# Two cross-attention layers: sharing one value product between two entries by turning every other entry's key order round

## The chip, the cores and the metric

The kernel runs on one core of a Trainium2 chip. The metric is the device time in microseconds of one execution; the time before is the median of three runs. A core has five engines that run their own instruction streams in order and wait for each other by semaphores: TensorE (PE, matrix products; its weight loads are shown as PEld), VectorE (DVE), ScalarE (ACT), GpSimd (POOL) and SyncE (SP), which here only issues DMAs.

## The reference

Sixteen batch entries go through two cross-attention layers. In the first one, which the change is about (the code counts it as layer 0), each entry has 256 queries of 320 channels (20 heads of 16) and 256 context rows of 512. The first 77 rows are text, the other 179 are image tokens.

```
q = hidden_states @ Wq
k_text, v_text = text @ Wk, text @ Wv;  ip_k, ip_v = ip @ Wk_ip, ip @ Wv_ip
probs = softmax(q_h @ k_h^T * scale)                      # per head, over the 77 text rows
text_out = probs @ v_h
text_probs = softmax(q @ k_text^T * scale)                # over all channels at once
sem = (text_probs @ text) @ ip^T * scale
ip_probs = softmax(q_h @ ip_k_h^T * scale + 0.5 * sem) * spatial_mask   # over the 179 image rows
out = (text_out + ip_probs @ ip_v_h) @ Wout + bout + residual
```

The second layer is of the same kind, with 252 text rows and 4 image rows and a normalised semantic term.

## The kernel before

Products are made in three terms: each fp32 operand is split into a rounded half ("high") and the rest ("low"), and high x high, high x low and low x high are added. `prod` (L240) issues these as 12 matmuls when 512 rows of contraction are four tiles of 128. ACT makes the high half with a copy, DVE or POOL the low half with a subtraction (`halves`, `split`, `evacuate`, `in_turn`).

Context is loaded for two entries at once (a pair, number c), four tiles (`cta`, `cta`, `ctb`, `ctb`) of 128 x 512, each for 128 of the 512 context channels, columns in the order text, image of the first entry, then of the second. From it come per pair the keys (`keys0`, `keys_first` for pair 0: text keys with weights `wk0` in `wA`, image keys with `wki0` in `wB`), and per entry:

- the values (`values0_`): three groups of `prod` with 128 context rows on the output's rows and 320 value columns. Group 0 is the text (weights `wC`, rows 0 to 127), group 1 is the image weights (`wD`) on the same rows 0 to 127, group 2 is the image weights on rows 128 to 255. Group 0 and 1 are masked by `tmask` (row below 77, or from 77 on) as ACT copies them into `vr`; so text and image share the first tile of 128 keys, the mixed tile;
- the text x image product `M` (`tokens0`, 77 x 179, made 192 wide) for the semantic term, and from it with the text probabilities `tph` a second use in `semantic0`.

The heads are worked on in groups of four, NG = 5 groups an entry, one group a slot, 80 slots k = 0 to 79 in the first layer. In slot k PE makes scores for the maxima (`score0`, L745, two slots ahead; DVE reduces them, L746 and L747), turns the maxima round (`maxima0`, L753), makes transposed scores (`turned0`, L769, keys on the rows, two tiles t = 0 and 1) which ACT exponentiates (L772) and POOL multiplies by the semantic factor `rs` (L775), and for slot k-1 sums the values (`attend0`, L804). `settle0` normalises on DVE and adds text and image parts on POOL into `hsn` (L822); after the fifth group POOL also copies the last half column block beside itself (L824), since the last 64 channels stand twice for the three-term product of the output. `gather` then transposes and `close0` projects (`ho`, L610).

The stacked operands `ks` and `qs` hold the keys and queries of four heads with 80 more rows (M and indicators for the semantic term, or maxima). They come by DMA from DRAM copies `kd` and `qd`, written from `kst` and `q`. There are four of each in turn, so a slot's stack is loaded four slots ahead. The queries of an entry (`queries0`) begin with a split of x into `hq` (L283 to L285), whose third low half DVE makes with a multiply-add.

The order on PE is written by hand: slots call their parts in turn, and `task` gives each step of the other work a due time in slots, which `fill` obeys. The start (`begin`) is written by hand for every engine; after it the compiler's scheduler orders ACT, DVE, POOL and SP.

Of the kernel before, what the change touches and what calls it, by code (L numbers as in the profile page):

```python
# [17 lines left out]
S = 256  # L18
H = 20
# [16 lines left out]
CH = H * D  # L36

# [14 lines left out]
def xattn2(  # L52
# [60 lines left out]
    words, slots = {"ctb": 1024, "cta": 1024, "raw": 512, "rawc": 512, "both": 2 * (S - T0), "kb": 936, "si": 256, "sp": 128, "wC": 2 * 4 * (H * D + NIP), "mt": S, "mx": 2, "tmp": (NG + 1) * 48, "kst": 4 * S, "rs": 2 * S, "P": 4 * S}, {}  # L113
# [47 lines left out]
    def halves(hi, lo, src, eng=nc.vector, loaded=False):  # L161
        order = queued if loaded else lambda inst: inst
        if len(hi.shape) != len(src.shape):
            src = src.rearrange("p (d h) -> p d h", d=D)[:, :, :H]
# [26 lines left out]
    def in_turn(parts, wait, tag="raw", eng=nc.vector, later=False):  # L191

        ahead, parts, tags = [], list(parts), tag.split()
        for i in range(len(parts) + 1):
# [4 lines left out]
            if i:  # L199
                halves(*ahead.pop(0), eng, wait)  # L200
# [52 lines left out]
    def evacuate(hi, lo, out, m):  # L253

        if m < 2:
            return halves(hi, lo, out)
        hi, lo = hi[:64], lo[:64]
        both = buf("both", list(hi.shape), bufs=2)
        nc.scalar.copy(hi, out[:64])
        nc.scalar.copy(both, out[64:])  # L260
        nc.vector.tensor_sub(out[:64], out[:64], f(hi))
        nc.vector.tensor_add(lo, out[:64], both)

    def context(b, n, wait=0):

        tiles, parts = [], []
        for k in range(0, 4, 3 - n):
            src = cT_d[:, b * S : (b + n) * S].rearrange("(k p) t -> p k t", p=128)[:, k : k + 3 - n]
            ct = buf("cta" if n == 1 or k < 2 else "ctb", [128, 2, 512], FR, bufs=SIZES["CTA" if n == 1 or k < 2 else "CTB"], name="ct")
            split = lambda t: t.rearrange("p (k t) -> p k t", t=n * S)  # L270
            parts.append((src, split(ct[:, 0]), split(ct[:, 1])))
            tiles.append(ct)
        yield from in_turn(parts, wait, "rawc raw" if b == 2 and n == 2 else "rawc", nc.gpsimd if wait and b != 2 else nc.vector, n == 2 and b > 2)
        if n == 2:
            return lambda s, k: tiles[k][:, s].rearrange("p (b t) -> p b t", b=2)
# [3 lines left out]
    def split(src, neg, eng, tag):  # L279
# [5 lines left out]
        order(nc.vector.scalar_tensor_tensor(hl[:, 2], f(hl[:, 2]), neg, src[:, 2], op0=ALU.mult, op1=ALU.add))  # L285
        return hl

    ct = [buf(t, [128, 2, 512], FR, bufs=2, name="ct") for t in ("cta", "cta", "ctb", "ctb")]
    ct0 = {0: lambda s, k, tiles=ct: tiles[k][:, s].rearrange("p (b t) -> p b t", b=2)}
# [10 lines left out]
    for k in range(4):  # L300
        first["c", k] = cT_d[k * 128 : (k + 1) * 128, : 2 * S], ct[k][:, 0], ct[k][:, 1], ("rawc", "raw")[k // 2]
# [8 lines left out]
    ks = [const_tile([128, 4, S], f"ks{i}", FR) for i in range(SIZES["NR"])]  # L310
# [8 lines left out]
    def constants():  # L319
# [3 lines left out]
        for i in range(SIZES["NR"]):  # L323
            nc.gpsimd.memset(f(ks[i]), 0.0)
# [1139 lines left out]
```

## Time and profile before

| | |
|---|---|
| median of 3 runs (range) | 1501.86 us (1500.63 to 1506.5) |
| profiled execution, its span | 1499.52 us, 1497.7 us |
| busy PE, DVE, ACT, POOL | 95%, 78%, 59%, 81% of the span |
| granted PE clock, mean | 0.984 |
| first layer's attention begins, at about | 56 us |
| PE busy from 300 to 400 us, and from 600 to 700 | 98.14 and 85.17 us of 100 |

The rows of the profile name the line of the kernel, the engine, the operation, output and input tiles and their shapes. "Idle before" is the time the engine stood still ahead of the instruction, with what released it. Matmuls overlap, so what one costs is read from the distance of two starts, not from its own duration.

### The profile page before, as it was taken

Reading aid. Unit: us, or ns where it says so; the run is one execution under the profiler, and the core shown is the slowest. Engines: PE = TensorE matmul, PEld = TensorE weight load, DVE = VectorE, ACT = ScalarE, POOL = GpSimd, SP = SyncE. Lnnn points to the kernel's source line nnn. Section 1 sums busy time; section 2 is a strip of 40 time slices with the busy share of each in tenths; the row PEclk is TensorE's granted clock in tenths of the full one; section 3 lists DMA queues with packets and bytes.
Section 4 is the critical chain, followed back from the end, with each engine's and each line's share of the span. In section 5 each row is a group of like instructions: output and inputs, shape, how many; then the busy total and the mean of one; then the engine's idle time right before and its main releaser. Section 6 shows DMA issues by size and latency. Waiting matters only on the chain.

```text
span 1497.7 us, 36123 instructions
## 1 busy us (share of the span) xinstructions
PE 1427.8 (95%) x12740; PEld 1155.6 (77%) x12740; DVE 1170.2 (78%) x2593; ACT 884.8 (59%) x1975; POOL 1215.2 (81%) x1304
## 2 busy tenths in 40 slices
PE   8789999999999899789999999999999999999997
PEld 8678888888888778577777777777777777777765
DVE  5467777777777787878887788778877887788785
ACT  5346565656565555556666666666666666666562
POOL 4259797979797977887698879887988798879786
PEclk9799999999999999999999999999999999999999
DMA  7767787778787776775434434443444344433411
GB/s 237 201 185 217 201 228 200 217 206 224 199 231 193 219 200 173 186 216 150 145 102 132 127 108 128 127 127 108 127 128 127 109 126 129 127 108 103 122 26 39
DMA packets 230986, 234.32 MB, mean 156 GB/s; under 512 B 39127, under 2 KB 200678, under 8 KB 230790
## 3 DMA queue, kind: packets, MB, share of 16 engines
q1 hardware_dynamic: 228598, 230.71, 55.4%
q8 instruction: 102, 1.67, 0.5%
q10 hardware_dynamic: 2208, 1.30, 0.4%
q14 instruction: 78, 0.64, 0.1%
HBM read 118.04 MB, written 77.04 MB: 130 GB/s over the span
## 4 chain that ended last, share of the span: by engine, by line
PE 73%; DVE 8%; DMA 6%; POOL 6%; issue 3%; ACT 3%; SPq 1%; ACTq 0%; DVEq 0%; POOLq 0%
PE X L942 15%; PE X L240 14%; PE P L804 6%; PE X L610 5%; PE P L954 5%; PE S L745 5%; PE P L964 4%; PE T L769 4%; PE T L894 3%; PE S L900 3%; PE X L613 2%; PE X L250 2%; PE X L579 2%; POOL P L775 2%; DVE mn L747 1%
## 5 line engine op out<-in xcount | busy, mean ns | idle before, releaser
L775 POOL TENSOR_TENSOR P<-P,rs 128x512 f32<-128x512 f32 x320 | 414.4, 1318 | 90.2 <-ACT P L772 89.3
L933 POOL TENSOR_TENSOR wt<-P,ctb 128x512 f32<-128x512 f32 x320 | 410.6, 1308 | 72.8 <-ACT ctb L932 72.8
L942 PE MATMUL X<-ctb,gm 128*128 128x512 f32 x1120 | 305.4, 402 | 5.8 <-DVE wt L943 5.7
L772 ACT ACTIVATE P<-T 128x512 f32<-128x512 f32 x320 | 175.4, 594 | 159.5 <-PE T L769 101.9
L943 DVE TENSOR_TENSOR wt<-X,wt 128x512 f32<-128x512 f32 x320 | 216.1, 680 | 42.7 <-PE X L942 36.4
L942 PEld LDWEIGHTS X<-ctb,gm 128*128 128x128 f32 x1120 | 195.3, 188 | 39.0 <-DVE wt L943 8.7
L914 ACT ACTIVATE P<-T 128x512 f32<-128x512 f32 x320 | 173.0, 593 | 76.2 <-PE T L894 73.3
L932 ACT ACTIVATE ctb<-P 128x512 fp32r<-128x512 f32 x320 | 186.7, 627 | 36.8 <-PE X L942 33.1
L902 DVE TENSOR_REDUCE mn<-S 128x4 fp32r<-128x1008 f32 x160 | 191.3, 1196 | 0.0
L747 DVE TENSOR_REDUCE mn<-S 128x4 fp32r<-128x716 f32 x160 | 142.2, 889 | 0.0
L804 PE MATMUL P<-P,vr 128*32 128x256 f32 x1920 | 127.4, 396 | 5.3 <-DVE tmp L821 2.0
L745 PE MATMUL S<-ks,qs 125*128 125x256 f32 x640 | 117.7, 307 | 4.9 <-DMA ks<-M 2.8
L745 PEld LDWEIGHTS S<-ks,qs 125*128 125x128 f32 x640 | 89.0, 195 | 40.1 <-issue 20.9
L1031 POOL TENSOR_TENSOR r<-u,rs 128x40 f32<-128x40 f32 (+2 forms) x17 | 108.7, 6394 | 3.9 <-DVE u L1028 3.9
L769 PE MATMUL T<-qs,ks 127*128 127x256 f32 x640 | 108.2, 292 | 0.4 <-DMA qs<-mt 0.4
L746 DVE TENSOR_REDUCE mn<-S 128x4 fp32r<-128x308 f32 x160 | 74.4, 465 | 31.2 <-PE S L745 30.8
L815 DVE STREAM_TRANSPOSE nt<-P 128x512 f32<-128x512 f32 x80 | 56.9, 711 | 51.8 <-PE P L804 51.3
L769 PEld LDWEIGHTS T<-qs,ks 127*128 127x128 f32 x640 | 92.1, 198 | 2.0 <-DMA qs<-mt 1.0
L804 PEld LDWEIGHTS P<-P,vr 128*32 128x32 f32 x1920 | 57.2, 112 | 47.0 <-issue 8.1
L954 PE MATMUL P<-P,v1t 128*32 128x256 f32 x1280 | 85.7, 385 | 0.0
L964 PE MATMUL P<-wt,zone 128*32 128x256 f32 x1280 | 85.1, 381 | 0.3 <-DVE wt L943 0.3
L610 PE MATMUL X<-ho,wF 128*128 128x256 f32 x512 | 74.3, 287 | 6.5 <-ACT mt L755 4.0
(297 smaller groups left out, 2974.5 us busy)
## 6 DMA issues: line engine op xcount, KB each, us to landing
qd<-q SPq DMA_DIRECT2D x96, 256.0 KB
qs<-tph SPq DMA_DIRECT2D x64, 320.0 KB
rawc<-in_cT_dram SPq DMA_DIRECT2D x60, 256.0 KB
qs<-qd SPq DMA_DIRECT2D x80, 192.0 KB
ks<-kd SPq DMA_DIRECT2D x80, 192.0 KB
ks<-kd SPq DMA_DIRECT2D x160, 96.0 KB
qs<-qd SPq DMA_DIRECT2D x160, 96.0 KB
kd<-kst SPq DMA_DIRECT2D x57, 256.0 KB
```

The costliest lines, as they stand in the source:

```text
L240: last = mm(out, lhs(a, k), rhs(b, k), start=i == 0, stop=i == len(terms) - 1)
L745: mm(sp[:, h], Q[: XROW + T0, h, t * 128 : (t + 1) * 128], K[: XROW + T0, h], start=True, stop=True)
L769: mm(st[p][:, j], K[:KS0, 2 * p + j, t * 128 : (t + 1) * 128], Q[:KS0, 2 * p + j], start=True, stop=True)
L772: exp = anchor(nc.scalar.activation(pt, st[p], AF.Exp, scale=SCALE))
L775: anchor(nc.gpsimd.tensor_mul(pt, pt, rs[:, t : t + 1].to_broadcast([128, 2, S])))
L804: mm(pv[32 * s : 32 * s + 32, o : o + S], v[:, vt, h : h + 32], P[k, s // 2][:, t, s % 2], start=vt < 2, stop=vt != 1,)
L902: anchor(nc.vector.tensor_reduce(maxes[k + 2][:, t], sp[:, :, :T1], axis=AX.X, op=ALU.max))
L914: anchor(nc.scalar.activation(P[k, u][:, t], st[u], AF.Exp, scale=SCALE))
L932: nc.scalar.activation(R[k, u][:, t], P[k, u][:, t], AF.Copy, scale=0.5)
L933: anchor(nc.gpsimd.tensor_sub(W[k, u][:, t], P[k, u][:, t], f(R[k, u][:, t])))
L942: mm(yp, gm[:, gb], R[k, u][:, kt], start=i == 0, stop=i == len(blocks[n]) - 1)
L943: nc.vector.tensor_mul(W[k, u][:, n], yp, W[k, u][:, n])
```

## The change

Nothing that is computed changes. Entries of even number get their keys, values and scores in the order image, text; odd ones keep text, image. A context tile is laid out as 51 zero columns, then for the high and then the low half: text of both entries (154), image of the even entry (179), a gap of 26 zeros, image of the odd entry (179), one zero. Rows 128 to 178 of the even entry's image, the gap, and rows 0 to 50 of the odd entry's image now lie 128 in a row, so one group of `prod` (`values_mixed`, task `vm`) makes the image values of both mixed tiles; ACT copies its result twice, with the mask of each entry. The even entry's mask is a new tile `emask`; the mask column of `vr` is written for each entry (`mark`) and no longer once at the start (`marks`). The keys' stack serves both orders from the same bytes, as one text block more stands behind the four heads (`turned_ks`), whose indicator rows need one more DMA for each of the four stacks at the start. `M` is laid out so that its zero columns are written once, and it is made 180 wide.

Since a layout has gaps, some operations come in two pieces: the halves of a context tile (text, image), the image part of a key's evacuation (each entry), the copy of the text keys to `kt`. Apart from that, `settle0` makes the last group's sum twice wide on DVE (in the second layer `settle1` its product), so POOL's copy (and in the first layer its add) goes, and for x the third low half of 64 rows moves from DVE to POOL.

```diff
+MIX = S - T0 - 128
+CI = 2 * T0
+CG = 128 + T0
+CW = CI + CG + S - T0 + 1
...
-    def evacuate(hi, lo, out, m):
+    def evacuate(hi, lo, out, m, pieces=None):
+        cut = [lambda t, b=b: t[:, b] for b in pieces] if pieces else [lambda t: t]
...
+        for of in cut:
+            nc.scalar.copy(of(hi), of(out[:64] if m == 2 else out))
...
+    def side(t, s, at, n):
+        at += MIX + s * CW
+        return t[:, at : at + n]
+    def texts_of(t, s):
+        return side(t, s, 0, CI).rearrange("p (b t) -> p b t", b=2)
+    def images_of(t, s, more=0):
+        return side(t, s, CW - 2 * CG, 2 * CG).rearrange("p (b t) -> p b t", b=2)[:, :, CG - S + T0 - 1 : CG - 1 + more]
...
+        if neg is None:
+            order(eng.tensor_sub(hl[64:, 2], src[64:, 2], f(hl[64:, 2])))
+        else:
+            order(nc.vector.scalar_tensor_tensor(hl[:, 2], f(hl[:, 2]), neg, src[:, 2], op0=ALU.mult, op1=ALU.add))
...
-    ks = [const_tile([128, 4, S], f"ks{i}", FR) for i in range(SIZES["NR"])]
+    ksw = [const_tile([128, 4 * S + T0], f"ks{i}", FR) for i in range(SIZES["NR"])]
+    ks = [by_head(t[:, : 4 * S]) for t in ksw]
+    turned_ks = [by_head(t[:, T0:]) for t in ksw]
...
+        for t in ct:
+            nc.gpsimd.memset(f(t[:, :MIX]), 0.0)
+            for s in range(2):
+                nc.gpsimd.memset(f(side(t, s, CI + S - T0, CG - S + T0)), 0.0)
+                nc.gpsimd.memset(f(side(t, s, CW - 1, 1)), 0.0)
...
+    def mark(b):
+        V = vr[(b + 2) % 3]
+        for t, m in enumerate(masks(b)):
+            nc.gpsimd.tensor_copy(vcols(V, V0W)[:, t, :, 16], m.to_broadcast([128, H]))
+        return V
...
             dma(ks[i][XROW + T0 : KS0, :, :T0], ind0r[:2, :T0].unsqueeze(1).to_broadcast([2, 4, T0]))
+            dma(ksw[i][XROW + T0 : KS0, 4 * S :], ind0r[:2, :T0])
...
-            for w, lo, hi, a, z in ((wk0, 0, T0 + 1, 0, T0), (wki0, T0 - 1, S, T0, S)):
+            for w, of, t in ((wk0, texts_of, T0), (wki0, lambda t, s: images_of(t, s, 1), S - T0 + 1)):
...
-        for t, (w,), lo, sc in ((0, wv0, 0, tmask[:, 0:1]), (1, wvi0, 0, tmask[:, 1:2]), (2, wvi0, 128, 1.0)):
+        value_rows(ct, T0 if i else -MIX, wv0[0], (V, 0, masks(b)[0]))
+        yield
+        value_rows(ct, CI + (CG + MIX if i else 0), wvi0[0], (V, 2, 1.0))
...
+    def values_mixed(c):
+        to = [(vr[(b + 2) % 3], 1, masks(b)[1]) for b in (2 * c, 2 * c + 1)]
+        value_rows(ct0[c], CI + 128, wvi0[0], *to)
+        yield
...
-        nc.gpsimd.memset(f(M[:, :, :T0]), 0.0)
-        prod(gp[:T0, : S - lo], lambda s, k: ct(s, k)[:, i, :T0], lambda s, k: ct(s, k)[:, i, lo:S], 4)
+        prod(gp[:T0, : S - T0 + 1], lambda s, k: texts_of(ct[k], s)[:, i], lambda s, k: images_of(ct[k], s, 1)[:, i], 4)
...
-        xs = split(x, tmask[:, 5:6], nc.gpsimd, "hq") if b else xs0.pop()
+        xs = split(x, None, nc.gpsimd, "hq") if b else xs0.pop()
...
-        Q, K = QK[k] = qs[k % SIZES["NR"]], ks[k % SIZES["NR"]]
+        Q, K = QK[k] = qs[k % SIZES["NR"]], (ks if b % 2 else turned_ks)[k % SIZES["NR"]]
...
-        for vt in range(3):
-            values0(k, pv, v, vt)
+        get("vm", b // 2)
+        for step in ((0, 0, 0, 1, 1), (1, 0, S, 1, 0), (2, 1, S, 0, 1)) if b % 2 else ((2, 0, S, 1, 0), (1, 1, S, 0, 1), (0, 1, 0, 1, 1)):
+            values0(k, pv, v, *step)
...
-        nc.gpsimd.tensor_add(hn[:, g // 2, :, g % 2], tmp[:, 0], tmp[:, 1])
         if g == NG - 1:
-            nc.gpsimd.tensor_copy(hn[:, 2, :, 1], hn[:, 2, :, 0])
+            nc.vector.tensor_add(hn[:, 2], *[tmp[:, i].unsqueeze(2).to_broadcast([128, 8, 2, 16]) for i in range(2)])
             later(0.45, lambda: gather(0, b))
+        else:
+            nc.gpsimd.tensor_add(hn[:, g // 2, :, g % 2], tmp[:, 0], tmp[:, 1])
...
-        task(("v0", 2 * c), shifted(n, -7, -5.4, -5), lambda b=2 * c: values0_(b), *k)
-        task(("v0", 2 * c + 1), shifted(n, -4, -3.8, -3.4), lambda b=2 * c + 1: values0_(b), *k)
+        task(("v0", 2 * c), shifted(n, -7, -5.4), lambda b=2 * c: values0_(b), *k)
+        task(("vm", c), shifted(n, -4.2), lambda c=c: values_mixed(c), *k)
+        task(("v0", 2 * c + 1), shifted(n, -3.8, -3.4), lambda b=2 * c + 1: values0_(b), ("vm", c))
```

How it moves instructions, at three places. On PE, in pair 4, between a slot's second `turned0` (output T) and the next slot's maxima (`ident_r`); wD is the image value weights, cta and ctb the context tiles. Before:

```order
737 L769 MATMUL T<-qs_97,ks_101 128x256 x4
738 L240 MATMUL X<-wD,cta_81 128x320 x3
739 L240 MATMUL X<-wD,cta_82 128x320 x3
740 L240 MATMUL X<-wD,ctb_83 128x320 x3
741 L240 MATMUL X<-wD,ctb_84 128x320 x3
742 L240 MATMUL X<-wD,cta_81 128x320 x3
743 L240 MATMUL X<-wD,cta_82 128x320 x3
744 L240 MATMUL X<-wD,ctb_83 128x320 x3
745 L240 MATMUL X<-wD,ctb_84 128x320 x3
746 L753 MATMUL X<-ident_r,mn_566 8x128 x2
```

And now (line numbers are those of the changed kernel):

```order
721 L864 MATMUL T<-qs_97,ks_101 128x256 x4
722 L251 MATMUL X<-wD,cta_81 128x320 x3
723 L251 MATMUL X<-wD,cta_82 128x320 x3
724 L251 MATMUL X<-wD,ctb_83 128x320 x3
725 L251 MATMUL X<-wD,ctb_84 128x320 x3
726 L848 MATMUL X<-ident_r,mn_614 8x128 x2
```

One of two groups is gone; the rest of PE's order around it stays, but that the odd entry's text group and the shared group change places a slot later.

On POOL, at the end of an entry (hq is the split of the next queries, P the probabilities, hsn the output being gathered). Before:

```order
260 L775 TENSOR_TENSOR P_122<-P_122,rs_115 128x512
261 L775 TENSOR_TENSOR P_123<-P_123,rs_115 128x512
262 L284 TENSOR_TENSOR hq_230<-xq_91,hq_230 128x512
263 L822 TENSOR_TENSOR hsn<-tmp_807 128x8x16
264 L775 TENSOR_TENSOR P_120<-P_120,rs_115 128x512
265 L775 TENSOR_TENSOR P_121<-P_121,rs_115 128x512
266 L824 COPY hsn<-hsn 128x8x16
267 L435 MEMSET M_260 77x2x77
268 L775 TENSOR_TENSOR P_120<-P_120,rs_115 128x512
```

And now:

```order
299 L397 COPY vr<-tmask 128x20 x2
300 L870 TENSOR_TENSOR P_123<-P_123,rs_116 128x512
301 L870 TENSOR_TENSOR P_124<-P_124,rs_116 128x512
302 L326 TENSOR_TENSOR hq_270<-xq_91,hq_270 128x512
303 L328 TENSOR_TENSOR hq_270<-xq_91,hq_270 64x256
304 L870 TENSOR_TENSOR P_121<-P_121,rs_116 128x512
305 L870 TENSOR_TENSOR P_122<-P_122,rs_116 128x512
306 L870 TENSOR_TENSOR P_121<-P_121,rs_116 128x512
```

The add, the copy and the memset are gone; two mark copies and the third low half stand there.

On ACT, its first copies in `begin`, with what they wait for (DMAHW: a load; Pool: GpSimd). Before:

```order
2 L1260 CAST cta_81<-rawc_117 128x512 [waits DMAHW0_49]
3 L1260 CAST wA_85<-P_120 128x320 [waits DMAHW1_49]
4 L1260 CAST cta_82<-rawc_118 128x512 [waits DMAHW2_49]
5 L1260 CAST wA_85<-P_121 128x320 [waits DMAHW3_49]
6 L1260 CAST ctb_83<-raw 128x512 [waits DMAHW4_49]
```

And now:

```order
2 L1359 CAST cta_81<-rawc_118 128x154 [waits DMAHW0_49]
3 L1359 CAST cta_81<-rawc_118 128x2x179 [waits Pool_49]
4 L1359 CAST wA_85<-P_121 128x320 [waits DMAHW1_49]
5 L1359 CAST cta_82<-rawc_119 128x154 [waits DMAHW2_49]
6 L1359 CAST cta_82<-rawc_119 128x2x179 [waits Pool_49]
```

Each context tile's copy is two, and the image one waits for POOL, which clears the gaps of that tile.

179 lines of the change are left out of this document (112 added, 67 removed).

## Prediction

> **What bounds the kernel now.** I read the page first (busy time), then the busy time by stretches, then what TensorE (PE) waited for, then the order of time on PE and GpSimd (POOL) in one period of the first layer, at last the first 60 us.
>
> ```profile
> span 1497.7 us, 36123 instructions
> PE 1427.8 (95%) x12740; PEld 1155.6 (77%) x12740; DVE 1170.2 (78%) x2593; ACT 884.8 (59%) x1975; POOL 1215.2 (81%) x1304
> ```
> ```profile
> 300.00:400.00 100.00, 98.14 (x933) 85.36 (x933) 78.11 (x182) 57.74 (x135) 85.61 (x84) 1.00 0.75 208
> ...
> 500.00:600.00 100.00, 91.32 (x842) 76.78 (x841) 81.77 (x183) 52.90 (x128) 80.71 (x89) 0.98 0.72 198
> 600.00:700.00 100.00, 85.17 (x785) 66.32 (x785) 77.20 (x173) 56.90 (x129) 86.58 (x100) 0.93 0.69 188
> ...
> 48.00:52.00 4.00, 2.33 (x17) 1.87 (x16) 1.29 (x2) 0.50 (x2) 0.23 (x1) 1.00 1.08 322
> 52.00:56.00 4.00, 0.47 (x3) 0.47 (x4) 3.10 (x6) 2.59 (x5) 0.00 (x0) 0.79 0.71 244
> ...
> 64.00:68.00 4.00, 4.00 (x27) 3.38 (x30) 1.32 (x3) 1.37 (x3) 2.01 (x2) 0.50 0.97 240
> ```
> The columns are the stretch, its length, busy us of PE, weight loads, VectorE (DVE), ScalarE (ACT) and POOL, the granted clock, DMA share and GB/s. From about 105 to 500 us, for which the first row stands, PE is busy all but 2%; from 500 to 700 it idles a tenth to a sixth; before 60 us it starves, and after the hole at 52 the clock is halved. What PE waits for in the dense part and in the hole-ridden one:
>
> ```profile
> PE X L610 <- ACT mt L755: 0.8, 1, 0.8
> PE X L240 <- DVE sp L670: 0.6, 1, 0.6
> PE X L667 <- DVE q L262: 0.3, 1, 0.3
> ```
> ```profile
> PE X L753 <- DVE mn L747: 4.2, 6, 1.7
> ```
> The first three rows are all of 200 to 300 us (1.7 us in 100), the last leads 500 to 600. So in the dense part each us taken off PE is a us of the kernel, if the engines that feed PE can follow; elsewhere it need not be.
>
> **The change, part by part.** One period of the dense part (a pair of entries), on PE:
>
> ```profile
> 262.54 1.13 PE L240 MATMUL X<-wC,cta 128*128 128x320 f32 x6
> ...
> 329.50 1.05 PE L240 MATMUL X<-wD,cta 128*128 128x320 f32 x6
> ...
> 332.15 1.04 PE L240 MATMUL X<-wD,ctb 128*128 128x320 f32 x6
> 333.03 0.28 PE L753 MATMUL X<-ident_r,mn 128*8 128x128 f32 x2
> ...
> 334.15 0.70 PE L240 MATMUL X<-cta 128*77 128x192 f32 x6
> 334.69 0.69 PE L240 MATMUL X<-ctb 128*77 128x192 f32 x6
> ...
> 337.94 1.13 PE L240 MATMUL X<-wC,cta 128*128 128x320 f32 x6
> ```
> A period is 337.94 - 262.54 = 75.4 us. 1) One value group of 12 matmuls goes per pair. From 329.50 to 333.03 stand two groups, so one is 3.53 / 2 = 1.765 us (not 12 times a matmul's own duration, since they overlap). Pairs 1 to 6 have it in the dense part: 6 x 1.765 = 10.6 us. Pair 7's lies at about 555 us, among PE's waits: between 0 and 1.8, taken as 0.9. Pair 0's lies at 46 us, ahead of the hole: nothing, that hole grows by it.
> 2) The token products go from 192 to 180 columns. Six take 334.69 - 334.15 = 0.54 us, 0.090 each; between no gain and full proportion (0.0056), taken at 0.005 x 12 x 14 entries = 0.8 us. Text keys from 156 to 154 columns: nothing.
> 3) POOL. Its rows, with those of DVE for the parts that change engines:
>
> ```profile
> L284 POOL TENSOR_TENSOR hq<-xq,hq 128x512 fp32r<-128x512 f32 x31 | 42.6, 1376 | 5.7 <-ACT hq L283 5.7
> L822 POOL TENSOR_TENSOR hsn<-tmp 128x128 f32<-128x128 f32 x80 | 41.0, 513 | 5.6 <-DVE tmp L821 5.1 <-DVE mx L674 0.5
> L824 POOL COPY hsn<-hsn 128x128 f32<-128x128 f32 x16 | 4.8, 300 | 0.1
> L435 POOL MEMSET M<- 77x154 f32 x16 | 3.6, 226 | 21.2 <-PE X L697 21.0
> L334 POOL COPY vr<-tmask 128x20 f32<-128x20 f32 x6 | 1.4, 302 | 3.9 <-DMA tmask<-in_tmask_dram 3.9
> ```
> ```profile
> L285 DVE SCALAR_TENSOR_TENSOR ho<-ho,tmask,hT 128x256 fp32r<-128x256 f32 x32 | 39.0, 1220 | 0.0
> L285 DVE SCALAR_TENSOR_TENSOR hq<-hq,tmask,xq 128x256 fp32r<-128x256 f32 x32 | 19.8, 618 | 2.3 <-ACT hq L283 1.9
> L168 DVE TENSOR_TENSOR q<-X,q 128x256 fp32r<-128x256 f32 x62 | 25.2, 415 | 12.1 <-ACT q L165 11.7
> ```
> Per pair POOL gains: two third low halves (256 columns; between 513 and 1376, by their middle width 0.8) = 1.6; four mark copies at 1.4 / 6 = 0.24: 1.0; each of four context tiles in two pieces (a line through 513 at 128 and 1376 at 512 has a foot of 0.23, so +0.2 each): 0.9; three key copies more: +0.2 each, 0.6. It loses two adds, two copies, two memsets: 2 x (0.51 + 0.30 + 0.23) = 2.1. Net +2.0 us on the 85.61 x 0.754 = 64.5 us of a period: 66.5 of 73.6, or 90%. POOL stays below PE on average, and its own waits are the cover. I look at where the cover is thinnest:
>
> ```profile
> 292.74 5.03 POOL L775 TENSOR_TENSOR P<-P,rs 128x512 f32<-128x512 f32 x4
> ```
> ```profile
> 298.17 1.50 PE L804 MATMUL P<-P,vr 128*32 128x256 f32 x24
> ```
> These four end at 297.77, and PE's attention starts 0.40 later; but its last 8 of 24 matmuls alone read the last two tiles, so the real slack is 0.40 + 1.50 x 16 / 24 = 1.4 us. In the run-up POOL now has one third low half and two half key copies more (0.8 + 0.3 or so). It fits, so I take 0; the bound is all of the 10.6. Even entries now read the late tiles after 8 matmuls instead of 16, which costs them 0.5 us of slack; in their slots POOL has idle time.
> 4) DVE loses 15 third halves (0.62 each) and gains 16 adds of 256 columns and three image pieces per pair (about 0.15 each), and in the second layer a doubled multiply. The add reads two SBUF tiles: between 0.42 (the q row, one input from PSUM) and 1.2 (the ho row, same size, both from SBUF); I take 0.8, so +7 us of DVE (16 x 0.8 + 24 x 0.15 - 15 x 0.62) where it is 78% busy. PE waits for DVE only from 500 to 700, with some 5 adds there: -1 to +3 us, taken as +0.5. The Trainium skill (SBUF — State Buffer, section "SBUF: two separate sides") says that a DVE instruction with two SBUF inputs and a POOL instruction that reads SBUF hold one port pair in turn, each for its whole length. The trace agrees: 1220 against 415 ns. By that rule the add costs 1.2 and the sum would end about 1 us later.
> 5) ACT gains about 11 short pieces per pair (0.15 each, 1.7 us of 75); it is 58% busy, and PE's one wait for it is 0.8 us per pair. Nothing.
> 6) Second layer: a POOL copy per entry goes; PE hides it but for the last entry: -0.3.
> 7) The start. Rows of POOL, ACT, PE, and SP's queue:
>
> ```profile
> 5.79 0.13 POOL L328 MEMSET vr<- 128x20 f32 x1
> ```
> ```profile
> 4.51 0.45 ACT L1260 CAST wA<-P 128x320 fp32r<-128x320 f32 x1
> ```
> ```profile
> 5.02 3.98 PE L401 MATMUL X<-cta,wA 128*128 128x156 f32 x16 [5.02 <-ACT wA L1260]
> ...
> 55.53 0.27 PE L753 MATMUL X<-ident_r,mn 128*8 128x128 f32 x1 [4.30 <-DVE mn L747]
> ```
> ```profile
> 4.97 0.48 SPq L85 DMA_DIRECT2D tmask<-in_tmask_dram  x1
> ...
> 17.24 3.17 SPq L85 DMA_DIRECT2D ks<-mt  x4
> ```
> In the new order ACT's first image piece waits for POOL's memsets of the gaps in that context tile, which stand behind the vr memsets. Those end at 5.92, plus 0.3 for larger ks memsets and some 0.3 for five small ones: 6.4. Behind the image piece (0.5) stands the copy of wA, done at 7.4 instead of 4.96, so PE starts 2.4 us later, into a chain in which PE, ACT and DVE take turns up to the hole. On SP four more DMAs stand ahead of the first stack loads, 0.48 (tmask) to 0.79 (3.17 / 4) each: +1.9 to +3.2. The two run beside one another, so +2.4, with ends 0 and 5.6 (all added). The wait of 4.30 at 55.53 is late by the same and 1.765 longer, since PE comes to it sooner.
>
> Sum: -10.6 - 0.9 - 0.8 - 0.3 + 0.5 + 2.4 = -9.7 us. The profiled execution took 1499.52 (span 1497.7), 2.3 below the median of the three runs, 1501.86. So 1489.8 for such a run, and 1492.2 against the median: 0.65% faster.
>
> **The rivals.** A) POOL can't follow. For it: 90% busy, and gap-free stretches in which the added pieces lie together. Against it: PE waits for POOL nowhere from 200 to 300, and 7 us of idle left in a period. If PE is held by what item 3 adds in each pair, up to 1.8 us each is lost: 1499 to 1503, no change.
> B) The clock. Rows 52 to 68 show that a hole of 4.30 us is followed by half clock, at which PE works full time. Longer holes before slot 0, or new ones from 500 to 700, would add two or three such stretches: 4 us of PE work at half speed is 2 us lost per 4 us stretch, so 4 to 7 us: 1496 to 1499. The Trainium skill (TensorE: Matmul & The Clock Gate, section "Part 1: The HAM clock gate (the "warmup" mystery)") gives a window of about 3.4 us; a hole that is already longer than that, as the one at 51, drops the clock once however long it gets. By that rule the start adds none of these, and only new holes would.
> C) Slower: operands at odd starts. Even entries' keys now start 77 elements into a tile, the image columns 205. Today's streamed operands start at even elements, so no row shows what an odd start costs PE. The nearest:
>
> ```profile
> L804 PEld LDWEIGHTS P<-P,vr 128*32 128x32 f32 x1920 | 57.2, 112 | 47.0 <-issue 8.1 <-POOL P L775 3.3 <-POOL wE L168 1.7
> L954 PEld LDWEIGHTS P<-P,v1t 128*32 128x32 f32 x1280 | 33.4, 109 | 24.8 <-issue 0.4
> ```
> ```profile
> L745 PE MATMUL S<-ks,qs 125*128 125x256 f32 x640 | 117.7, 307 | 4.9 <-DMA ks<-M 2.8 <-DVE mn L747 1.8
> L240 PE MATMUL X<-cta,wB 128*128 128x360 f32 x96 | 18.5, 328 | 0.6 <-DVE sp L670 0.6
> ```
> Weights of heads 17 wide start odd half the time, those 22 wide never: 112 against 109 ns, next to nothing. Touched would be half of L745 (59 us) and the image keys (18.5 for two of four tiles, so 37): 96 us. It cancels the gain at 10% more per matmul, and ends slower by over 0.5% (above 1509.4) from 18%; at 25% it is 1492 + 24 = 1516.
>
> **How the numbers follow.** Forecast 0.60 (1488 to 1497: start and POOL a little better or worse), A 0.20, B 0.13, C 0.07. A measurement here tells about 0.5% (7.5 us) from nothing. Below 1494.4: most of the forecast's case (0.55) and a little of A and B (0.03): 0.58. Slower: C and a mishap at the start, 0.08. The rest, 0.34, is the same. The range 1484 to 1501 takes in the forecast's case, most of A and all of B, and below it a start that costs nothing with pair 7's group in full.
>
> **What would show it.** Right: 96 fewer 128x320 matmuls; a period of 73.5 us instead of 75.4; PE still over 97% busy from 105 to 480 with no wait on L775 among its first; PE's first matmul at about 7.4 us and the first attention about 2 us later than now; the second layer as long as now. Wrong: a period near 75 with PE waiting for POOL's products (A), more stretches at 0.5 (B), or matmuls of the even entries' scores or of 360 columns that take longer than 307 and 328 ns (C).

## The result: 0.5% slower, where 0.65% faster was forecast

| | before | after |
|---|---|---|
| median (range), 19 runs each | 1499.29 us (1494.83 to 1509.76) | 1507.83 us (1499.28 to 1515.45) |
| after / before | | 1.0054, 95% interval 1.0038 to 1.0070 |
| profiled execution, its span | 1499.52 us, 1497.7 us | 1504.56 us, 1502.8 us |
| start of the value sums of slot 0, 5, 55 | 66.9, 118.4, 492.8 us | 71.3, 117.2, 495.0 us |
| first scores of the second layer | 677.0 us | 681.6 us |

The 96 matmuls are gone, and PE is idle instead. Every position in a trace below is that of one execution, and executions of one kernel spread widely (16.2 us for the 19 of the changed kernel), so the repeated slots and the medians carry the argument. The page's busy line and the stretches of the changed kernel, columns as in the prediction:

```profile
PE 1420.7 (95%) x12644; PEld 1143.8 (76%) x12644; DVE 1191.5 (79%) x2626; ACT 889.2 (59%) x2031; POOL 1217.4 (81%) x1358
...
300.00:400.00 100.00, 96.16 (x908) 81.49 (x900) 81.55 (x182) 57.49 (x140) 84.98 (x92) 1.00 0.78 206
...
500.00:600.00 100.00, 90.11 (x813) 76.78 (x812) 79.57 (x174) 53.39 (x135) 80.53 (x96) 0.95 0.73 197
600.00:700.00 100.00, 85.51 (x781) 64.81 (x780) 79.47 (x174) 54.22 (x123) 83.14 (x93) 0.95 0.72 187
```

What PE waits for from 200 to 300 us, after:

```profile
PE X L251 <- DVE sp L763: 2.1, 2, 1.1
PE S L839 <- DMA qs<-qd: 1.5, 1, 1.5
PE X L848 <- DVE mn L842: 0.4, 1, 0.4
PE X L706 <- ACT mt L850: 0.3, 1, 0.3
PE X L848 <- DVE kst L276: 0.2, 1, 0.2
```

4.5 us of waits stand where 1.7 stood. POOL's products (now L870) are not among them. Most new waits are in the same slot of every pair, so I cut each pair into its ten slots. A slot's length is the distance from its first maxima matmul (L753 before, L848 after) to that of the next; the table gives the median over slots 10 to 53 by k modulo 10 (slots 3, 5 and 7 move by at most 0.1 us in the kernels shown, and the sum is over all ten).

| slot of a pair | before | after | e1 | e5 | e7 | e13 | e14 |
|---|---|---|---|---|---|---|---|
| 0 | 8.87 | 9.21 | 8.87 | 9.22 | 8.87 | 8.91 | 9.01 |
| 1 | 6.10 | 6.49 | 6.10 | 6.46 | 6.10 | 6.13 | 6.13 |
| 2 | 8.66 | 8.26 | 10.60 | 8.25 | 8.67 | 8.26 | 8.26 |
| 4 (the group removed) | 7.81 | 6.03 | 6.05 | 6.03 | 6.05 | 6.03 | 6.44 |
| 6 | 8.67 | 10.27 | 9.97 | 8.64 | 8.67 | 10.17 | 8.64 |
| 8 | 7.58 | 7.46 | 7.42 | 8.22 | 7.57 | 7.80 | 7.99 |
| 9 | 6.90 | 8.22 | 6.96 | 8.21 | 6.88 | 8.21 | 6.91 |
| sum of ten | 74.5 | 75.9 | 75.9 | 75.0 | 72.8 | 75.3 | 73.2 |

The group's 1.78 us are saved in slot 4 (1.765 was forecast); slots 6, 9, 0 and 1 take 1.60, 1.32, 0.34 and 0.39 of it back. These are the three theories that the experiments test: D (slot 6, transfers that land late), O (slot 9, order on VectorE), and S, later sharpened to K (slots 0 and 1, the doubling add).

### The profile page after: what moved, and what is told of

Read it like the earlier page. It is cut to its first block, busy times and chain, and to the rows that moved or that the text cites. A ratio compares the mean times of both kernels' runs of the same rounds, so it can differ in the third digit from the quotient of the medians.

```text
span 1502.8 us, 36181 instructions
## 1 busy us (share of the span) xinstructions
PE 1420.7 (95%) x12644; PEld 1143.8 (76%) x12644; DVE 1191.5 (79%) x2626; ACT 889.2 (59%) x2031; POOL 1217.4 (81%) x1358
## 4 chain that ended last, share of the span: by engine, by line
PE 47%; DVE 5%; DMA 4%; POOL 4%; issue 2%; ACT 1%; SPq 1%; ACTq 0%; DVEq 0%; POOLq 0%
PE X L1038 15%; PE X L251 6%; PE P L1050 5%; PE P L1060 4%; PE X L703 3%; PE S L996 3%; PE T L990 3%; PE X L672 2%; PE X L706 1%; DVE wt L1039 1%; PE X L1169 1%; POOL P L870 1%; PE P L899 1%; PE X L261 1%; PE X L1016 1%
## 5 line engine op out<-in xcount | busy, mean ns | idle before, releaser
L870 POOL TENSOR_TENSOR P<-P,rs 128x512 f32<-128x512 f32 x320 | 415.2, 1319 | 106.4 <-ACT P L867 102.3
L1010 ACT ACTIVATE P<-T 128x512 f32<-128x512 f32 x320 | 173.2, 593 | 75.5 <-PE T L990 73.2
L839 PE MATMUL S<-ks,qs 125*128 125x256 f32 x640 | 118.4, 308 | 11.4 <-DMA qs<-qd 4.0
L271 ACT CAST kst<-X 128x179 fp32r<-128x179 f32 (+5 forms) x117 | 36.1, 329 | 82.6 <-PE X L251 44.7
```

The source lines that it names most:

```text
L839: mm(sp[:, h], Q[: XROW + T0, h, t * 128 : (t + 1) * 128], K[: XROW + T0, h], start=True, stop=True)
L870: anchor(nc.gpsimd.tensor_mul(pt, pt, rs[:, t : t + 1].to_broadcast([128, 2, S])))
L1010: anchor(nc.scalar.activation(P[k, u][:, t], st[u], AF.Exp, scale=SCALE))
```

## The experiments

Ratios are against the kernel before on the same chip, with 95% intervals. Each edit is of the changed kernel unless it says otherwise.

**Slot 6: the group's own saving.** e1 takes the group off the kernel before and changes nothing else; the tile gets the second group's values instead, so the output is not the reference's:

```diff
+            if t == 2 and i == 0:
+                yield
+                continue
...
-            nc.scalar.activation(vcols(V, V0W)[:, t, :, 0:16], ...
+            for u in (1, 2) if t == 1 and i == 0 else (t,):
+                nc.scalar.activation(vcols(V, V0W)[:, u, :, 0:16], ...
```

> The kernel before, with the even entry's third value group of each pair left out (12 matmuls of 320 columns less per pair; its tile is filled from the bank of the second group, so the output is not the reference's) and nothing else of the change. Theory P (the prediction's): between 105 and 500 us each us off PE is a us of the kernel, so about 6 x 1.77 + 0.9 = 11 us less than before, ratio 0.992 to 0.994. Theory D: the group stood in a stretch of about 12 us in which the DMA engines are at full share, so the next slot waits for its maxima rows instead and some 1.1 us per pair come back: about 4 us less, ratio 0.996 to 0.998.

Measured: 1.0093 (1.0061 to 1.0125). Less work on PE alone is slower. Theory P falls; D's sign for slot 6 is right (9.97 us), its size for the whole is not, because slot 2 lengthened too: there PE waits for the output projection's `ho`, since on DVE the transposes of `hT` that it is made from now stand behind the row maxima and no longer ahead. The slot that grows, in the changed kernel, PE rows:

```profile
339.07 0.28 PE L848 MATMUL X<-ident_r,mn 128*8 128x128 f32 x2
340.08 0.71 PE L839 MATMUL S<-ks,qs 125*128 125x256 f32 x4 [0.73 <-issue]
340.63 0.40 PE L864 MATMUL T<-qs,ks 127*128 127x256 f32 x2
341.37 0.47 PE L864 MATMUL T<-qs,ks 127*128 127x256 f32 x2 [0.34 <-DMA qs<-mt]
```

The same place by stretches, last two columns DMA share and GB/s, first before, then after, and SP's queue just ahead of it, after:

```profile
333.70:336.20 2.50, 2.50 (x35) 2.04 (x37) 1.46 (x3) 1.60 (x4) 0.92 (x1) 1.00 1.04 294
336.20:338.70 2.50, 2.50 (x27) 2.09 (x20) 2.00 (x4) 0.88 (x2) 1.80 (x3) 1.00 0.77 179
338.70:341.20 2.50, 2.50 (x21) 2.44 (x20) 2.25 (x8) 2.23 (x6) 2.50 (x2) 1.00 0.76 219
```
```profile
335.10:337.60 2.50, 2.50 (x32) 1.92 (x25) 1.75 (x4) 0.72 (x3) 2.47 (x4) 1.00 1.12 282
337.60:340.10 2.50, 1.77 (x15) 1.56 (x13) 2.39 (x7) 2.42 (x6) 2.30 (x2) 1.00 1.07 232
340.10:342.60 2.50, 2.16 (x15) 1.99 (x16) 1.29 (x2) 1.39 (x5) 2.42 (x3) 1.00 1.08 255
```
```profile
332.65 0.42 SPq L89 DMA_DIRECT2D xq<-in_xT_dram  x1
333.24 0.60 SPq L89 DMA_DIRECT2D qs<-tph  x1
333.89 0.60 SPq L89 DMA_DIRECT2D qs<-qd  x1
```

PE arrives earlier, the DMA engines are at their full share (1.07 to 1.12), and a 384 KB load of the odd entry's x stands ahead of the query stacks that PE needs. So e5, e6 and e7 issue that load 2.2 slots earlier, just ahead of 5 us with a DMA share of 0.32 to 0.51 in both kernels; PE's order stays as it was:

```diff
-        task(("q0", 2 * c + 1), shifted(n, -5.4, -4, -3, -2.8, -2), ...
+        task(("q0", 2 * c + 1), shifted(n, -7.6, -4, -3, -2.8, -2), ...
```

> The changed kernel, with the load of the odd entry's queries issued 2.2 slots earlier (due -7.6 instead of -5.4), out of the stretch in which the DMA engines are at full share and into one where they are half idle; PE's order is the same. Theory D (in the slot two after the removed group PE waits for the query stacks and maxima rows that land behind that load): the slot that grew from 8.67 to 10.27 us falls below 9.2, some 1.1 us per pair, 6 to 7 us less than the changed kernel, ratio 0.9995 to 1.002 against before. Rival L (that slot is held by the chain of four small transfers on ACT's queue, whatever SP moves): the slot stays above 9.7 and the ratio at 1.004 to 1.007.

Measured: 1.0033 (1.0010 to 1.0055), slot 6 at 8.64 us. Theory D holds for the slot, rival L falls; the ratio lies between the two ranges. Of the 1.6 us some return in slot 8, where PE waits twice in four pairs for ACT's copy `mt` (1.8 and 1.9 us).

> The kernel before with the same earlier load alone: the control. Theory D: there PE did not wait in that slot, so nothing to gain, its length stays 8.67, ratio 0.998 to 1.002. If the load at its old place had held the kernel before as well, or its new place costs something: outside of that.

Measured: 1.0029 (1.0007 to 1.0051), slot 6 at 8.67. The load was no limit before, as D says, but the control misses its bounds: its profiled execution, the second longest of twelve, loses 2.5 us at one place (at 216 us, PE waiting for `sp`) and 8 between 493 and 677 us.

> The kernel before without the even entry's third value group (as before, its tile filled from the second group's bank) and with the earlier load. Theory D: slot 6 of a pair falls from 9.97 to below 9.2, and the 2 us that the output projection waits in slot 2 depend on the order that the scheduler finds for ACT and VectorE; with that wait the ratio is 1.003 to 1.006, without it 0.994 to 0.997. Rival L: slot 6 stays, ratio 1.007 to 1.011 with the wait in slot 2.

Measured: 0.9951 (0.9931 to 0.9971). Every slot is as before but slot 4, which is 1.76 shorter. Against the kernel before that is 7 us, where the prediction's terms for the group sum to 11.5; but against e6, which has the same earlier load and all groups, it is 12.3 us (medians 1491.54 and 1503.83, the means 11.5 apart, give or take 3). So the price of the group was right once that load is out of the way; what the earlier load costs by itself, 1.0029 in e6, is not explained.

**Slot 9: the order on VectorE.** DVE's rows there, before, and then after, with the PE row that waits:

```profile
363.63 0.48 DVE L285 SCALAR_TENSOR_TENSOR hq<-hq,tmask,xq 128x256 fp32r<-128x256 f32 x1 [0.40 <-ACT hq L283]
364.03 0.23 DVE L670 TENSOR_TENSOR sp<-sp,X 128x77 f32<-128x77 f32 x1
...
364.52 0.47 DVE L746 TENSOR_REDUCE mn<-S 128x4 fp32r<-128x308 f32 x1
364.90 0.89 DVE L747 TENSOR_REDUCE mn<-S 128x4 fp32r<-128x716 f32 x1
```
```profile
365.40 0.89 DVE L842 TENSOR_REDUCE mn<-S 128x4 fp32r<-128x716 f32 x1
366.21 0.23 DVE L763 TENSOR_TENSOR sp<-sp,X 128x77 f32<-128x77 f32 x1
```
```profile
366.49 0.76 PE L251 MATMUL X<-cta,wB 128*128 128x360 f32 x3 [1.05 <-DVE sp L763]
```

The third low half (`hq`) is gone from DVE, and the scheduler now puts the maxima ahead of the sum `sp`, which holds the bank that the image keys need. e2 pins the old order:

```diff
-            nc.vector.tensor_add(sp, sp, sf[:, :T0])
+            seen[0] = nc.vector.tensor_add(sp, sp, sf[:, :T0])
...
-        nc.vector.tensor_reduce(mn[:, t, :, 0], sp[:, :, text], axis=AX.X, op=ALU.max)
+        queued(nc.vector.tensor_reduce(mn[:, t, :, 0], sp[:, :, text], axis=AX.X, op=ALU.max), seen[0])
```

> The changed kernel, with one thing more: on VectorE the sum of the text scores (sp) stands ahead of the row maxima of the second score tile, as in the kernel before, where in the changed kernel it stands behind them 6 times. Theory O: that swap costs PE a wait of about 1.1 us at the image keys of each pair, so 6 to 7 us less than the changed kernel, ratio 0.9995 to 1.0015 against before. Rival: what PE no longer waits for there it waits for at the next maxima, ratio 1.004 to 1.006 as the changed kernel.

Measured: 1.0057 (1.0029 to 1.0084). Slot 9 fell to 6.91 us as O says, but slot 0 rose from 9.21 to 10.21, where PE waited at the next maxima, and the rival has the total. The sum of the ten slots is still 1.1 us less than in the changed kernel; in the profiled execution that is lost again between slot 55 and the second layer.

Three runs undo parts. e3 takes the doubling and the third low half back, e4 puts only these two into the kernel before, e12 takes the third low half back and has the earlier load:

```diff
-        xs = split(x, None, nc.gpsimd, "hq") if b else xs0.pop()
+        xs = split(x, tmask[:, 5:6], nc.gpsimd, "hq") if b else xs0.pop()
...
-            nc.vector.tensor_add(hn[:, 2], *[tmp[:, i].unsqueeze(2).to_broadcast(...) for i in range(2)])
+            nc.gpsimd.tensor_copy(hn[:, 2, :, 1], hn[:, 2, :, 0])    # and POOL's add for all five groups
```

> The changed kernel with two parts undone: the output's last group in the first layer is doubled on POOL again, and the query split's third low half is made by VectorE again; layout, value group for both mixed tiles and the second layer's doubled multiply stay. Theory O: the order on VectorE is that of before (the sum of the text scores ahead of the maxima), so 6 to 8 us less than the changed kernel, ratio 0.999 to 1.001. Rival S (the side changes are worth what they take off POOL or DVE, and the layout's pieces cost the time): ratio 1.004 or more.

Measured: 1.0080 (1.0047 to 1.0113), in the range of rival S. Yet the slots are not what S says: 9, 0 and 1 are as before (6.92, 8.91, 6.13), as O says, and it is slot 2 that is 11.28: ACT's cast of `ho` starts 1.4 us after its input is there, behind a row of other short copies, and PE waits 1.25 + 0.46 us.

> The kernel before with the two side changes of the first layer alone (VectorE doubles the output's last group, GpSimd makes the query split's third low half), no change of layout and all six value groups. Here the sum of the text scores stands behind the maxima once, not six times. Theory O: near no change, ratio 0.999 to 1.002. Rival (the 256-column add, 16 x 0.4 to 1.0 us of VectorE, or POOL's third half costs the time by itself): ratio 1.004 to 1.008.

Measured: 1.0033 (1.0013 to 1.0053), between what the two expect; slots 0 to 9 are as before but for slots 1 and 8 (6.35 and 7.96 us, longer) and slot 2 (8.25, 0.41 shorter).

> The changed kernel with the earlier load and the query split's third low half on VectorE again; the doubling add stays on VectorE. Theory O: the sum of the text scores stands behind the maxima once instead of 6 times, slot 9 at 6.9 to 7.0 us instead of 8.2. Theory S: slots 0 and 1 stay at 9.2 and 6.5 or go beyond, since the adds are there. Ratio 0.999 to 1.002. If it was the third half itself that cost time, slots 0 and 1 fall too, ratio below 0.998.

Measured: 1.0098 (1.0073 to 1.0123), slot 9 at 10.63 us. The order of `sp` and the maxima was right again, so this wait had another cause, and it names it. DVE and POOL there:

```profile
293.24 3.50 DVE L330 SCALAR_TENSOR_TENSOR hq<-hq,tmask,xq 128x256 fp32r<-128x256 f32 x1 [0.26 <-ACT hq L325]
296.66 0.41 DVE L916 TENSOR_TENSOR tmp<-nt,P 128x256 f32<-128x256 f32 x1
296.99 0.22 DVE L763 TENSOR_TENSOR sp<-sp,X 128x77 f32<-128x77 f32 x1
```
```profile
289.98 5.01 POOL L870 TENSOR_TENSOR P<-P,rs 128x512 f32<-128x512 f32 x4
294.94 1.26 POOL L326 TENSOR_TENSOR hq<-xq,hq 128x512 fp32r<-128x512 f32 x1
296.15 0.31 POOL L467 CAST kb<-kst 128x154 fp32r<-128x154 f32 x1
```

An instruction of 0.48 us (row above) took 3.50, until POOL's gap-free row ended; `sp` stood behind it, and PE waited 2.6 us.

**Slots 0 and 1: the doubling add.** e8 combined the earlier load and the pinned order.

> The changed kernel with the earlier load and the sum of the text scores ahead of the maxima. Theories D and O together: slot 6 below 9.2 us and slot 9 at 6.9 instead of 8.2, the 1.1 us of each, 12 us less than the changed kernel, ratio 0.996 to 0.999; the waits of slots 0 and 1 that came with the second of these (1.3 us) take it back to 0.999 to 1.003 if they stay. Rival (PE only waits elsewhere): 1.004 or more.

Measured: 1.0032 (1.0011 to 1.0054). Slot 9 at 6.92, slot 6 at 9.04, slot 0 at 9.57. There, DVE, POOL and PE:

```profile
304.20 2.77 DVE L918 TENSOR_TENSOR hsn<-tmp 128x256 f32<-128x256 f32 x1
306.90 0.58 DVE L276 TENSOR_TENSOR kst<-X,kst 128x179 fp32r<-128x179 f32 x2
```
```profile
303.93 2.51 POOL L870 TENSOR_TENSOR P<-P,rs 128x512 f32<-128x512 f32 x2
```
```profile
307.63 0.28 PE L848 MATMUL X<-ident_r,mn 128*8 128x128 f32 x2 [1.56 <-DVE kst L276]
```

The doubling add took 0.41 us at some places, up to 1.38 in the first layer's slots of the changed kernel, and 2.77 here, through two products of POOL; the image keys wait behind it, and the bank that the next maxima need is theirs. e9 takes the add back to POOL (the second hunk of the edit above) beside the earlier load:

> The changed kernel with the earlier load, and with the first layer's last output group doubled on POOL again (the third low half stays with GpSimd). The adds on VectorE took 0.42 us where POOL had just ended an instruction and up to 2.8 us where it was in one. Theory S (these adds delay the evacuation of the image keys and the maxima behind them): slots 0 and 1 of a pair fall from 9.2 and 6.5 us to 8.9 and 6.1; with D and O slot 6 is 8.7 and slot 9 is 6.9, slot 4 stays 6.0. If slot 2 is below 8.8, some 8 us less between 118 and 493 us than before, less the start's 4: ratio 0.995 to 0.998; if the order on ACT and VectorE makes the output projection wait in slot 2 (10.6 to 11.3 us, as in two earlier runs), 1.000 to 1.004. Rival: slots 0 and 1 stay at 9.2 and 6.5, ratio 0.999 to 1.003.

Measured: 1.0107 (1.0072 to 1.0141). Slot 1 at 6.13 as S says, slot 0 at 9.11 with waits for the maxima's transfers instead, and waits for `ho` in slots 2 and 7; the ratio is beyond all three of its ranges. The longest of that kind is in e11, which has the start's edit too; DVE, POOL, PE:

```profile
351.80 8.18 DVE L326 TENSOR_TENSOR ho<-hT,ho 128x512 fp32r<-128x512 f32 x1
```
```profile
351.01 2.23 POOL L174 TENSOR_TENSOR cta<-rawc,cta 128x358 fp32r<-128x358 f32 x3
353.17 4.96 POOL L870 TENSOR_TENSOR P<-P,rs 128x512 f32<-128x512 f32 x4
358.08 1.35 POOL L174 TENSOR_TENSOR ctb<-rawc,ctb 128x154 fp32r<-128x154 f32 x2
```
```profile
360.04 1.86 PE L703 MATMUL X<-ho,wF 128*128 128x256 f32 x7 [5.31 <-DVE ho L326]
```

A subtraction that takes 0.67 us elsewhere took 8.18: it came through when POOL's nine instructions, the layout's context pieces among them, had ended. That gave theory K, and e13 tests it with no work moved: the add keeps its place, but reads one input from PSUM.

```diff
+            two = tmp[:, 0], pv[:, S : S + 128].rearrange("p (f d) -> p f d", d=16)
+            for a in range(2):
+                nc.vector.tensor_mul(two[a], nt[:, a, :, 0:16], rzw[:, a])
+            nc.vector.tensor_add(hn[:, 2], *[t.unsqueeze(2).to_broadcast([128, 8, 2, 16]) for t in two])
```

> The changed kernel, in which the doubling add of the last group reads one input from PSUM and one from SBUF instead of both from SBUF (the multiply ahead of it is cut in two for that, about 0.1 us more of VectorE); nothing is moved to another engine. Theory K (a VectorE instruction with two SBUF inputs lasts until POOL's running instruction ends: the add took 0.42 to 1.4 us in the changed kernel, up to 2.9 in others, and the ho subtraction 8.2 us in a gap-free stretch of POOL): the adds fall to 0.45 us throughout, and slots 0 and 1 of a pair to about 8.9 and 6.1 us; some 0.7 us per pair, ratio 1.001 to 1.004. Rival W (the add costs by its work and its place, wherever its inputs are): slots 0 and 1 stay at 9.2 and 6.5.

Measured: 1.0020 (1.0004 to 1.0037), slots 0 and 1 at 8.91 and 6.13. The groups of the add, changed kernel and e13 (mean ns of one):

```profile
L918 DVE TENSOR_TENSOR hsn<-tmp 128x256 f32<-128x256 f32 x16 | 15.3, 959 | 0.4
```
```profile
L923 DVE TENSOR_TENSOR hsn<-tmp,P 128x256 f32<-128x256 f32 x16 | 6.6, 412 | 0.2
```

Theory K is shown for the add, W falls: what costs is that both inputs are in SBUF while POOL runs. In e13, 11 of the 16 adds run beside a POOL instruction from start to end and still take 0.40 to 0.42 us.

**The start, and all repairs together.** e10 writes the gaps' zeros ahead of the key stacks' (`for t in ct: ...` moved to the head of `constants`). PE's first rows, after and e10:

```profile
7.30 3.89 PE L484 MATMUL X<-cta,wA 128*128 128x154 f32 x16 [7.30 <-ACT wA L1359]
```
```profile
5.02 4.01 PE L484 MATMUL X<-cta,wA 128*128 128x154 f32 x16 [5.02 <-ACT wA L1359]
```

> The changed kernel with POOL's memsets of the context tiles' gaps ahead of those of the key stacks; nothing else. PE's first matmul at 5 to 5.5 us instead of 7.3. Theory T (the start's delay is paid once and stays): the first attention 2 to 4 us earlier, and the kernel as much, ratio 1.002 to 1.004. Rival C (the dip of the clock behind it takes the difference, as the first five slots did in the changed kernel, 4.4 us late at slot 0 and 1.2 early at slot 5): ratio 1.004 to 1.007 as the changed kernel.

Measured: 1.0057 (1.0035 to 1.0079). The first matmul is 2.3 us earlier, the first value sum only 1.1 (70.2 against 71.3), and e13 and e14 without this edit have it at 70.4 and 70.2. The whole shows no gain: the ratio is in C's range, though its interval reaches the upper end of T's.

> The earlier load, the last output group doubled on POOL, and the gaps' memsets first: all that the theories find wrong with the change, at once. Theories D, S, O and T: 2 to 4 us less than with the first two alone, ratio 0.992 to 0.996, faster than both kernels. Rival C: as with the first two alone, within 1 us.

Measured: 1.0100 (1.0061 to 1.0139); the row of 8.18 us is why.

> The changed kernel with the earlier load, the sum of the text scores ahead of the maxima, and the add reading PSUM. In the run without the last of these the adds took up to 2.8 us in slot 0 and PE waited 0.5 to 1.6 us there for the evacuation of the image keys behind them. Theories D, O and K: slot 0 at 8.9, 1 at 6.1 to 6.2, 2 at 8.3, 4 at 6.0, 6 at 8.7 to 9.0, 9 at 6.9, so some 2 us per pair less than before, less the start's 4: ratio 0.994 to 0.998. Rival: some other queue's order makes PE wait, as it did in four of the runs so far; then 1.000 or more, and the table by slots shows which.

Measured: 0.9983 (0.9966 to 1.0000), between its two ranges. Its period is 73.2 us (prediction 73.5), and the value sums of slot 55 start at 482.9, 9.9 us ahead of before. By the second layer 4.0 are left. (The profiled execution, 1492.14 us, is the second shortest of twelve; the median is 1495.2.) The largest single loss, DVE and PE:

```profile
503.48 3.30 DVE L549 TENSOR_TENSOR rawc<-rawc 64x512 f32<-64x512 f32 x1 [1.51 <-POOL P L870]
```
```profile
508.13 1.27 PE L251 MATMUL X<-cta,wB 128*128 128x360 f32 x3 [4.16 <-DVE sp L763]
```

> As the run before it, with the gaps' memsets first. Theory T: 2 us less than that run. The first such comparison (ratio 1.0057 against 1.0054 of the changed kernel) spoke for rival C: the same within 1 us.

Measured: 0.9975 (0.9948 to 1.0001). The medians are 1495.9 and, in e14, 1495.2: nothing of T's 2 us shows, but less than some 3 us can't be told here.

e16 and e17 move that square to POOL in e14 and e15, e18 in the kernel before:

```diff
-        nc.vector.tensor_mul(sq, cipn, cipn)
+        nc.gpsimd.tensor_mul(sq, cipn, cipn)
```

> The changed kernel with the earlier load, the sum of the text scores ahead of the maxima, the add reading PSUM, and the one square of the second layer's image tokens (64x512, two SBUF inputs) on POOL instead of VectorE. That square took 1.25 us in the kernel before and 3.3 to 3.5 in the kernels with the new layout, while POOL ran without a gap, and PE waited 4.2 us behind it in the run without this edit. Theory K: that wait goes, 2 to 4 us less than that run (ratio 0.9983), so 0.994 to 0.997, faster than both kernels. Rival: the next such instruction or POOL's own added 0.8 us take the place, 0.998 or more.

> As the run before it, with the gaps' memsets first. Rival C so far: the start's 1 to 2 us at the first attention are not found again at the end; the same within 2 us either way. Theory T: 1 to 2 us less.

> The kernel before with the square on POOL alone: the control for the run with all repairs. In the kernel before the square took 1.25 us and PE's waits next to it are 0.8 to 1.7 us. Theory K: at most 1 us, ratio 0.998 to 1.001. If the repair gained as much here as there, the new layout would have no part in it.

Measured: 1.0001 (0.9976 to 1.0026), 1.0003 (0.9977 to 1.0030) and 1.0009 (0.9985 to 1.0034). The wait of 4.16 is gone, and the ratios of e16 and e17 are those of the rival. In e16 PE now waits 5.1 us for the next step behind this square, DVE's product L559. POOL's part of it ended at 517.7 us, but on DVE the product stands behind two subtractions that wait for copies of ACT:

```profile
519.43 0.42 DVE L276 TENSOR_TENSOR q<-X,q 128x256 fp32r<-128x256 f32 x1 [2.66 <-ACT q L271]
521.70 0.32 DVE L276 TENSOR_TENSOR kst<-X,kst 128x154 fp32r<-128x154 f32 x1 [1.84 <-ACT kst L271]
521.93 0.23 DVE L559 TENSOR_SCALAR rawc<-ident,rn 64x64 f32<-64x64 f32 x1
```
```profile
522.32 0.65 PE L562 MATMUL X<-rawc 64*128 64x64 f32 x2 [5.10 <-DVE rawc L559]
```

In the profiled executions e16 and e17 are 6.9 and 12.7 us ahead at slot 55 and 3.7 and 2.3 us behind at the second layer. No run of the correct kernels is measurably faster than before; e14 and e15 come nearest.

## Why the prediction was wrong

The step that failed is the "if" in "each us taken off PE is a us of the kernel, if the engines that feed PE can follow". The prediction tested it on POOL's rows and on busy shares; transfers and the order on DVE have no term in the sum. Per pair, 1.78 us were saved in slot 4 and 3.65 taken back: 1.60 in slot 6 by a load ahead of the query stacks (e5), 1.32 in slot 9 by DVE's order (e2, e8, e14), 0.73 in slots 0 and 1, nearly all by the adds (e13). With all three repaired (e14) the period is 73.2 us, where 73.5 was forecast. At slot 55 the changed kernel is 2.2 us behind, where items 1, 2 and 7 add up to some 9 ahead (an estimate); what it loses behind that, up to 8.5 us in the medians, is not explained.

- **What bounds the kernel, and item 1.** The size of the group was right (1.78 for 1.765). PE's 98% showed that nothing else made it wait at today's pace; it did not show how far the next limit was. Two slots on, the query stacks and maxima rows came too late for a PE that arrived earlier, and moving one load cured it (e1, e5, e7). The quoted row of 300 to 400 us had a DMA share of 0.75 in the mean; its 2.5 us stretches went up to 1.05. A full share alone makes no wait: at 368.7 to 371.2 us before, with 1.05, PE was busy all 2.50. I had noted where POOL's cover is thinnest, and not where that of the transfers is.
- **Item 3, POOL at 0.** PE indeed doesn't wait for L870 from 200 to 500 us, and I stopped at that. POOL's work holds up DVE's instructions with two SBUF inputs, and PE waits for what stands behind these. So rival A has a part of the truth, with DVE in the middle: 0.73 of the 3.65 us. The forecast +2.0 us of POOL a pair does not show: POOL is busy 84.98 us of 100 from 300 to 400, for 85.61.
- **Item 4, DVE at +0.5.** The price of the add was fair in the mean (0.96 for 0.8), and the sentence from the Trainium skill (SBUF — State Buffer, section "SBUF: two separate sides"), that such an instruction and one of POOL's hold the port pair in turn, agrees with the rows of the add: 0.40 to 0.42 us with one input in PSUM, 0.41 to 2.91 without. DVE as a whole is busy 21.3 us more (1191.5 for 1170.2), not 7. What failed here is the weighing: I counted busy time, and placed it where I took PE to wait before. That reading was wrong too: of the three waits shown for 200 to 300 us two are for DVE, `sp` (0.6) and `q` (0.3), and the one for `sp` is the one that grew in slot 9. What counts is who is queued behind the one long instance: slots 0 and 1 pay 0.73 us a pair for it, of which e13 brings back 0.66. Nor had I asked what the scheduler does with DVE's order once `hq` is out: slot 9, 1.32 us a pair (e2).
- **Item 5, ACT at nothing.** Near right in the changed kernel: slot 8's waits for `mt` are 0.3 to 0.6. (Slot 2 gains 0.41, but so it does in e4 with the old layout, so this comes from the side changes.) In e3 and e5 ACT's order cost PE waits of about 1.7 and 1.0 us a pair.
- **Item 2** holds: six products take 0.51 us instead of 0.54.
- **Item 6.** -0.3 was forecast; between 677 and 765 us the changed kernel loses 3.0, after that little up to the last entries. What this is, no run tells. The end is shorter: from the value sums of the second layer's slot 75 on it takes 53.2 to 53.7 us in all runs made from the changed kernel, and 54.2 to 57.4 in those made from the one before.
- **Item 7.** First matmul at 7.30 (forecast 7.4); first value sum 4.4 us late, within the ends but not at the forecast 2.4. Little of it comes from the first matmul, as e10 shows, where 3.3 of it stay; from what else, no run tells. The wait of 4.30 came 3.8 us later and was 4.63, longer by 0.33, not by 1.765. By slot 5 PE was 1.2 us early: the clock from 97.5 to 104 us, 0.59 in the mean before, was 1.00. Neither e10 nor e15 nor e17 shows anything of the start's delay in the whole time, within some 3 us.
- **Rivals B and C.** The mean granted clock is 0.982 for 0.984; counted in steps of 0.5 us, there are eight stretches at half clock, 50.5 us in all, where there were seven, 44.5 us: at most 3 us, so not B in the main. For C, the groups of the two signs that the prediction named (307 and 328 ns before):

```profile
L839 PE MATMUL S<-ks,qs 125*128 125x256 f32 x640 | 118.4, 308 | 11.4 <-DMA qs<-qd 4.0 <-DMA ks<-kd 3.7 <-DMA ks<-M 2.0
L251 PE MATMUL X<-cta,wB 128*128 128x360 f32 x96 | 20.3, 349 | 9.0 <-DVE sp L763 9.0
```

Means mix in waits and the half clock. From start to start (medians), the scores of the even entries take 124.0 ns where they took 119.0, those of the odd ones 119.0 as before, and the matmuls of 360 columns 168.5 ns for 165.0. So C is there, at 2 to 4%, where it needed 10% to cancel the gain: some 2 us, an estimate from 320 x 5 and 192 x 3.5 ns. That the odd starts are the reason is not shown.

What stays open: from slot 55 (493 us before) to the second layer the profiled executions of e13 to e17 lose 6 to 15 us against before, while e5 loses none. e18, one instruction apart from the kernel before, loses 4 there, and was 5 behind already at slot 55, ahead of that instruction. The waits there differ from run to run, and no run separates the scheduler's order from what single executions of one kernel differ by.

## What to carry to other kernels

A busy share near 100% says that an engine is the pace, not that it is the only one: before counting a saving, look in the slots behind it for the transfer or chain that lands last, and at its share in stretches as short as a slot. Price an added instruction by its longest instance and by what is queued behind it. Where a scheduler sets the order, moving one instruction off an engine reorders the rest; pin the two or three orders on which the bound engine hangs.

## What was not expected of the hardware

A DVE instruction with two SBUF inputs at some places waited not for one POOL instruction but for a whole gap-free row of them: 3.50 us for 0.48, 8.18 for 0.67, and the square of 64x512 took 1.25 us before and 3.48 after at the same place. The new layout is not needed for that: in e1, which has the old one, the square took 3.27 us, and in e7 0.72. Nor does every row keep DVE out: in the kernel before POOL runs from 338.5 to 375.6 us without a gap of 0.1 us, and in it such instructions took 0.48 us (`hq`) and 1.66 (`ho`); the changed kernel's adds of 1.05 to 1.38 us came in after one POOL instruction. What decides between the two, no run tells. With one input in PSUM the add never stretched (16 adds of 0.40 to 0.42 us).
